# Two fused attention blocks on one core: layer norms, context loads and row tests moved between engines

## The chip, the cores and the metric

The kernel runs on one core of a Trainium2 chip. The core has a matrix engine (TensorE, PE in the profile; its weight loads are shown as PEld), a vector engine (VectorE, DVE), an activation engine (ScalarE, ACT), a general engine (GpSimd, POOL) and a sync engine (SyncE, SP), from whose queue nearly all DMAs of this kernel are issued. [...] Every engine works through its own queue in order, and engines wait for each other through semaphores. The metric is the device time of one execution in microseconds; a time is given as the median of several runs.

## What is computed

Sixteen sequences of 256 rows and 512 columns go through two transformer blocks. All arithmetic is in float32.

```python
# block 0
q = layer_norm(x) @ q_w ; k, v = split(layer_norm(ctx) @ kv_w)      # 16 heads of 32
x = x + softmax(q k^T * scale, masked) v @ proj_w + proj_b
x = x + gelu(layer_norm(x) @ fc1_w + fc1_b) @ fc2_w + fc2_b         # 512 -> 2048 -> 512
# block 1
mask0 = 1 - all(x == 0, axis=2)
x1 = layer_norm(x + mha(x, x, mask0, causal)) * g1 + b1
mask1 = 1 - all(x1 == 0, axis=2)
x2 = layer_norm(x1 + mha(x1, ctx, mask1)) * g2 + b2
z = (relu(x2 @ f1^T + b) * mask0 @ f2^T + b') * mask0
out = layer_norm(x2 + z) * g3 + b3
```

Two details matter below. `mask0` and `mask1` ask of every row whether it has a nonzero element. In the cross attention the context rows are multiplied with `mask1` before keys and values are made of them.

## The kernel before

**Tiling.** The sixteen sequences are worked on as eight groups (`NG`), each of two sequences, that is 512 rows, or four tiles (`G`) of 128 rows by 512 columns. A float32 product is made of three matmuls over a high and a low part (`mm3`); hence each operand is first "split": one engine copies it to the rounded high part and DVE or POOL subtracts to get the low part (`split`, L127 to L133; `split_lazy`, L139 to L142).

**Stages in order of time.** First comes block 0's attention (up to about 690 us). Then comes the first MLP (`Mlp0`): its first half "up" (512 to 2048, to about 1082 us) and its second half "down" (2048 to 512, to about 1458 us), both with a Strassen scheme of seven products, where sums of quarter matrices replace the eighth product. Block 1 follows: eight self attention jobs (job 0 to 7, about 66 us each), eight cross attention jobs (job 8 to 15, about 76 us each) and the second MLP from about 2600 us.

**The order of work.** PE's order is written out by hand (`tc.manual_schedule(engines={PE})`). On the other engines' queues and on SP the framework places the instructions when the kernel is built, by a simulated time line and by the program's order. In attention, `weave` interleaves two streams on PE: the attention of one job (scores, transposes of the exponentials, weighted sums) and the `feed` of the next job (its projections, transposes of its input rows, and the loads of weights). So `feed(8)`, which prepares the first cross job, runs beside the attention of job 7.

**Norms in block 1.** When half a job (one sequence) is done, two calls of `norm` are put in a list, and one of them is emitted per head. `norm` calls `layer_norm(..., True)`: the statistics on DVE (L238 to L241), the power -0.5 on POOL (L242), then the normalizing in one DVE pass (L252) and gain and offset in two POOL passes (L253, L254). For a self job DVE then tests the row for nonzero elements (`nonzero`, L1225, with an output tile `junk` that nobody reads), which gives `m1`. Then the rows are stored to DRAM (L1298). The third norm, in the second MLP, uses the two fused DVE passes L256 and L257 instead.

**Context rows.** `context(n, t)` loads tile t of the context (L1408), multiplies it by `m1` on POOL (L1409) and has PE transpose it (L282). It is called in the feed of a cross job: tiles 0 and 1 after the first of four projections, tile 2 after the second and tile 3 after the third (`FRONTS`). The row tiles `cx` share the three buffers of the tag `t512` with `junk` and, in the second MLP, with `relu` and `y`.

**The first MLP, down.** It runs over 32 steps: four per group of rows (q = 0 to 3), each with seven products of twelve matmuls. In each step `sums_down` makes four sums for the next step: `differences` puts s1 and s3 on POOL (L796, L798) and s2 and s4 on DVE (L797, L799). After each product its operand slot is rewritten for the next step (`write`: a copy on ACT, L141, and a subtraction on DVE, L142). The residual rows `x` are loaded at q = 1 (q = 2 in the first group), and the second bias is added to them on POOL (`offset`, L1042) at q = 2 (q = 3 in the first group). In a group's last step `end` adds the products into these rows on DVE and POOL; it then stores them and tests each of the four row tiles for nonzero elements with `nonzero` on DVE, into `m0`.

**The first MLP, up.** Its four sums per group go through the same `differences`. At its start (`begin`) all four sums and the seven low parts are made on POOL, and the high parts by DVE copies (L860).

## Time and profile before

| What | us |
|---|---|
| median of three runs (2823.62 to 2831.68) | 2824.41 |
| the profiled execution | 2834.77 |
| its span, first to last instruction | 2832.9 |
| PE idle between matmuls, down (1082 to 1458) | 34.1 |
| the same, cross attention (1970 to 2600) | 42.2 |
| the same, up (690 to 1082) | 24.0 |
| the same, self attention (1482 to 1970) | 4.4 |

The idle times are sums of PE's gaps above 0.15 us in the trace. The mean granted clock of PE is 0.981 of full speed. In the profile an engine's line reads: line of the code, engine, operation, output<-inputs, shapes and count; in a list of waits it reads "who waited <- for whom: us in total, times, longest". In a timeline the first two columns are the start in us and the length, and brackets at the end give the idle time of the engine just before, with what ended it. `SPq` marks the issue of a DMA, not its transfer. An idle engine costs nothing unless it makes the end later.

### The profile page before, as it was taken

What the parts mean: (1) busy time and instruction counts of PE and PEld (TensorE: products, weight loads), DVE (VectorE), ACT (ScalarE), POOL (GpSimd) and SP (SyncE); (2) the same over time, 40 slices, a digit from 0 to 9 for tenths busy, and PEclk for the clock granted to TensorE, in tenths of its full rate; (3) what the DMA queues carried; (4) which work ended last, traced back from release to release, by engine and by line L of the source; (5) the groups of instructions that cost most, each with busy time, mean ns of one, the idle gap of its engine ahead of it and who ended that gap; (6) DMA issues with size and microseconds to landing.
All of it is one profiled execution on the core that took longest, in us unless ns stands there. A gap on an engine that the chain in (4) does not pass through costs nothing.

```text
span 2832.9 us, 56614 instructions
## 1 busy us (share of the span) xinstructions
PE 2683.6 (95%) x18970; PEld 2261.0 (80%) x18970; DVE 2047.1 (72%) x5801; ACT 1794.4 (63%) x5221; POOL 942.1 (33%) x963
## 2 busy tenths in 40 slices
PE   7999999998899999899989999999889999999998
PEld 5777777776799999899977888887767777777787
DVE  7666666757746568888876777777667777777887
ACT  4877777778455555333337878787667777777532
POOL 6122211204501125545551222335233323324533
PEclk9999999999999999999999999999999999999999
DMA  7565555654323344434366565667556555556321
GB/s 229 168 192 177 174 176 168 193 157 139 128 110 132 120 149 164 149 120 150 132 230 189 180 190 182 191 197 238 160 187 193 174 182 185 176 161 181 99 93 60
DMA packets 287809, 465.41 MB, mean 164 GB/s; under 512 B 36256, under 2 KB 188320, under 8 KB 279328
## 3 DMA queue, kind: packets, MB, share of 16 engines
q1 hardware_dynamic: 287520, 461.78, 51.3%
q8 instruction: 153, 2.51, 0.4%
q14 instruction: 136, 1.11, 0.1%
HBM read 284.97 MB, written 176.69 MB: 163 GB/s over the span
## 4 chain that ended last, share of the span: by engine, by line
PE 70%; DVE 13%; DMA 6%; issue 4%; ACT 3%; POOL 3%; SPq 0%; POOLq 0%; DVEq 0%; ACTq 0%
PE ps_p L263 18%; PE ps_v L263 15%; PE ps_pt L454 9%; PE ps_z L473 6%; PE ps_s L413 5%; PE down L1025 5%; PE up_sc L912 4%; DVE c_t L142 3%; PE up_pt L912 2%; PE up_mm L912 2%; PE ps_t L282 2%; ACT e L438 1%; DMA d<-qk 1%; DVE st L238 1%; PE ps_e L1253 1%
## 5 line engine op out<-in xcount | busy, mean ns | idle before, releaser
L438 ACT ACTIVATE e<-e,mn 128x256 f32<-128x256 f32 (+1 forms) x1024 | 487.7, 480 | 69.3 <-DVE mn L428 67.7
L460 ACT COPY pt<-ps_pt 128x512 f32<-128x512 f32 (+1 forms) x696 | 378.0, 546 | 161.8 <-PE ps_pt L454 150.7
L454 PE MATMUL ps_pt<-ident,e 128*128 128x128 f32 x2816 | 437.4, 274 | 11.7 <-ACT pt L460 6.0
L454 PEld LDWEIGHTS ps_pt<-ident,e 128*128 128x128 f32 x2816 | 336.7, 141 | 52.3 <-ACT pt L460 12.4
L413 PE MATMUL ps_s<-stack 97*128 97x256 f32 (+1 forms) x1536 | 331.7, 297 | 16.8 <-ACT e L438 13.3
L413 PEld LDWEIGHTS ps_s<-stack 97*128 97x128 f32 (+1 forms) x1536 | 269.0, 190 | 72.6 <-ACT e L438 18.3
L1329 POOL TENSOR_TENSOR x<-x,zz 128x256 f32<-128x256 f32 x128 | 95.5, 746 | 592.5 <-DVE zz L1322 577.5
L438 ACT ACTIVATE e<-ps_s,mn 128x256 f32<-128x256 f32 x512 | 241.0, 483 | 79.1 <-DVE mn L424 50.2
L1025 PE MATMUL down<-w_h,c_t 128*128 128x256 f32 x900 | 261.8, 292 | 24.0 <-DVE c_t L142 24.0
L1025 PE MATMUL down<-w_h,x_t 128*128 128x256 f32 x868 | 252.5, 291 | 9.4 <-ACT x_t L141 7.8
L1025 PE MATMUL down<-w_l,x_t 128*128 128x256 f32 x868 | 251.3, 289 | 0.0
L428 DVE CUSTOM_DVE_ANT_0 e<-mb,ps_s 128x256 f32<-128x256 bf16 x512 | 192.7, 415 | 77.8 <-PE ps_s L413 75.7
L242 POOL TENSOR_TENSOR rstd<-rstd,nhalf 128x1 f32<-128x1 f32 x192 | 123.3, 649 | 332.9 <-DVE rstd L241 286.4
L473 PE MATMUL ps_z<-pt,v 128*32 128x256 f32 (+1 forms) x3072 | 212.3, 376 | 10.1 <-DVE zs L651 3.6
L263 PE MATMUL ps_p<-x_t,q_h 128*128 128x512 f32 x640 | 217.0, 420 | 3.6 <-DVE x_t L133 1.7
L424 DVE TENSOR_REDUCE mn<-ps_s 128x2 f32<-128x512 f32 x256 | 174.9, 683 | 51.4 <-PE ps_s L413 48.3
L428 DVE CUSTOM_DVE_ANT_0 e<-tri,ps_s 128x128 f32<-128x128 f32 (+1 forms) x512 | 158.6, 345 | 61.2 <-PE ps_s L413 58.9
L1025 PEld LDWEIGHTS down<-w_h,c_t 128*128 128x128 f32 x900 | 178.3, 198 | 27.6 <-DVE c_t L142 27.6
L438 ACT ACTIVATION_READ_ACCUMULATOR e<-e,mn 128x1 f32 x1024 | 197.8, 193 | 0.0
L141 ACT CAST x_t<-sums 128x512 fp32r<-128x512 f32 x152 | 90.4, 618 | 154.4 <-DVE sums L797 84.6
L1025 PEld LDWEIGHTS down<-w_h,x_t 128*128 128x128 f32 x868 | 172.6, 199 | 11.6 <-ACT x_t L141 9.8
L473 PEld LDWEIGHTS ps_z<-pt,v 128*32 128x32 f32 x3072 | 86.0, 111 | 115.0 <-issue 29.4
(248 smaller groups left out, 7632.0 us busy)
## 6 DMA issues: line engine op xcount, KB each, us to landing
stack<-d SPq DMA_DIRECT2D x1152, 128.0 KB
d<-qk SPq DMA_DIRECT2D x192, 512.0 KB
hid<-ho SPq DMA_DIRECT2D x32, 1024.0 KB
raw<-hid SPq DMA_DIRECT2D x32, 1024.0 KB
x<-xd SPq DMA_DIRECT2D x128, 256.0 KB
xd<-x SPq DMA_DIRECT2D x96, 256.0 KB
xin<-in_x_dram SPq DMA_DIRECT2D x32, 256.0 KB
xin<-in_ctx_dram SPq DMA_DIRECT2D x32, 256.0 KB
```

What stands on the lines that cost most here:

```text
L242: nc.gpsimd.tensor_tensor(out=rstd[:, 1:2], in0=rstd[:, 0:1], in1=nhalf, op=ALU.pow)
L263: nc.tensor.matmul(ps, w[p], x[q], start=(k == 0 and i == 0), stop=(k == kc - 1 and i == 2))
L413: nc.tensor.matmul(ps[:, t, :], u.st[: self.rows, 0, j, ts(t, P)], u.st[: self.rows, 1, j, :], start=True, stop=True,)
L424: nc.vector.tensor_reduce(mn, ps, AX.X, ALU.min)
L428: nc.vector.tensor_tensor_reduce(out=e[:, at], in0=bias[t], in1=ps[:, t, : job.width[t]], scale=-SC, scalar=BIG, op0=ALU.add, op1=ALU.min, ...
L438: nc.scalar.activation(e[:, at], ps[:, t, :] if bias is None else e[:, at], AF.Exp, bias=mn[:, t : t + 1], scale=-1.0, accum_out=u.rs[:, t ...
L454: nc.tensor.transpose(pp[:, ts(x, P)], e[:, at : at + P], ident)
L460: nc.scalar.copy(pt[:, :n], pp[:, :n])
L473: nc.tensor.matmul(z[ts(j, D), w[0] * P :], job.v[u.i * NT + mc][:, u.c * P + j * D : u.c * P + (j + 1) * D], u.pt[j][:, x0 * P : (x0 + le ...
L912: nc.tensor.matmul(ps[:, mm, :], w[p][:, k, :], x[q][:, k, :], start=(first and mm == k == j == 0), stop=(k == 1 and j == 2), skip_group_c ...
L1025: nc.tensor.matmul(ps[:, t, :], x[p][:, mm, ts(t, P)], w[r][:, bo, :], start=(q == mm == t == j == 0), stop=(q == self.NS - 1 and mm == 1 ...
L1329: nc.gpsimd.tensor_tensor(out=xv, in0=xv, in1=zz, op=ALU.add)
```

## The change

It has several parts, in all of which the results stay the same up to rounding:

- `layer_norm` loses its pooled form. The norms of block 1 take two fused passes on DVE: (x - mean) * gain, then x * rstd + offset.
- Context rows are loaded by a new function `context_rows`, apart from `context`. After the keys of a job's feed, tiles 0 to 2 of the next job are loaded if that is a cross job, or tiles 0 and 1 if it is the first cross job. Inside `context(n, t)`, once tile t is transposed, tile t + 3 is loaded. A tile not yet loaded is loaded just before its use.
- `Mlp0.end` no longer calls `nonzero`. ACT takes the absolute values of a row tile and accumulates their sum into `m0`; one DVE operation on four columns then turns the sums into 0 or 1.
- In `differences` s4 goes to POOL in every case.
- `offset` is called at q = 3 for all groups.
- `write` in `begin` copies the high part on ACT instead of DVE, and subtracts on POOL as before.

```diff
-    def layer_norm(pool, x, gain, offset, pooled=False):
+    def layer_norm(pool, x, gain, offset):
         mean, rstd = ln_stats(pool, x)
-        if pooled:
-            nc.vector.tensor_scalar(x, x, mean, rstd, ALU.subtract, ALU.mult)
-            nc.gpsimd.tensor_tensor(out=x, in0=x, in1=gain, op=ALU.mult)
-            nc.gpsimd.tensor_tensor(out=x, in0=x, in1=offset, op=ALU.add)
-        else:
-            nc.vector.scalar_tensor_tensor(x, x, mean, gain, ALU.subtract, ALU.mult)
-            nc.vector.scalar_tensor_tensor(x, x, rstd, offset, ALU.mult, ALU.add)
+        nc.vector.scalar_tensor_tensor(x, x, mean, gain, ALU.subtract, ALU.mult)
+        nc.vector.scalar_tensor_tensor(x, x, rstd, offset, ALU.mult, ALU.add)
...
             own.tensor_tensor(out=s2, in0=s1, in1=a11, op=ALU.subtract)
             pool.tensor_tensor(out=s3, in0=a11, in1=a21, op=ALU.subtract)
-            own.tensor_tensor(out=s4, in0=a12, in1=s2, op=ALU.subtract)
+            pool.tensor_tensor(out=s4, in0=a12, in1=s2, op=ALU.subtract)
...
-            if own is None:
-                split_lazy(self.a[i], h, l, nc.vector)
-            else:
-                nc.vector.tensor_copy(h, self.a[i])
-                own.tensor_tensor(out=l, in0=self.a[i], in1=h.bitcast(F32), op=ALU.subtract)
+            split_lazy(self.a[i], h, l, own or nc.vector)
...
                 for t in range(G):
                     junk = self.flat("junk").rearrange("p m n -> p (m n)")
-                    nonzero(junk, x[:, t, :], m0[:, g, t : t + 1])
+                    nc.scalar.activation(
+                        junk, x[:, t, :], AF.Abs, accum_out=m0[:, g, t : t + 1]
+                    )
+                nc.vector.tensor_scalar(m0[:, g, :], m0[:, g, :], 0.0, None, ALU.not_equal)
...
-                elif q == (2 if g else 3):
+                elif q == 3:
                     self.offset(xs[g])
...
-                layer_norm(pool, x, table[:, 0, :], table[:, 1, :], True)
+                layer_norm(pool, x, table[:, 0, :], table[:, 1, :])
...
+        cxs = {}
+
+        def context_rows(n, t):
+            if n < len(jobs) and jobs[n].cross and (n, t) not in cxs and t < G:
+                cx = cxs[n, t] = pool.tile([P, C], F32, tag="t512", name="cx", bufs=3)
+                nc.sync.dma_start(out=cx, in_=of("ctx", jobs[n].g)[:, t, :])
+
         def context(n, t):
...
-            cx = pool.tile([P, C], F32, tag="t512", name="cx", bufs=3)
-            nc.sync.dma_start(out=cx, in_=of("ctx", job.g)[:, t, :])
+            cx = cxs[n, t]
             nc.gpsimd.tensor_scalar(cx, cx, job.m[:, t : t + 1], None, ALU.mult)
-            return transposed(job.c_t, cx, t)
+            cost = transposed(job.c_t, cx, t)
+            context_rows(n, t + 3)
+            return cost
...
                     for t in FRONTS[c]:
+                        context_rows(n, t)
                         yield context(n, t)
...
             weight(n + 1, "k")
+            for t in range(3 if n + 1 > NG else 2):
+                context_rows(n + 1, t)
```

## The prediction

> **What bounds the kernel now.** I read the page's busy shares first, then the waits of TensorE, then busy time and granted clock by stage, and then the timeline at the longest waits. PE is busy for 2683.6 of 2832.9 us, so only a shorter PE idle time, or a higher granted clock, can shorten the run.

> ```profile
> PE 2683.6 (95%) x18970; PEld 2261.0 (80%) x18970; DVE 2047.1 (72%) x5801; ACT 1794.4 (63%) x5221; POOL 942.1 (33%) x963
> ...
> PE ps_t L282 <- POOL cx L1409: 24.6, 2, 12.9
> PE down L1025 <- DVE c_t L142: 24.0, 16, 3.5
> PE ps_s L413 <- ACT e L438: 13.3, 7, 2.7
> ...
> 1082.00:1458.00 376.00, 342.46 (x2697) 336.48 (x2696) 321.95 (x406) 140.00 (x244) 203.07 (x144) 0.96 0.41 141
> 1482.00:1970.00 488.00, 483.17 (x3493) 390.91 (x3492) 359.72 (x1677) 381.67 (x1331) 143.57 (x155) 1.00 0.64 196
> 1970.00:2090.00 120.00, 95.37 (x674) 75.58 (x673) 74.29 (x271) 72.99 (x242) 45.77 (x43) 0.89 0.58 184
> 2090.00:2600.00 510.00, 491.88 (x3505) 387.56 (x3505) 381.56 (x925) 368.49 (x1197) 166.21 (x168) 0.99 0.59 178
> ```

> The stage rows give length, busy PE, PEld, DVE, ACT and POOL, the granted clock, DMA. They are the first MLP's second half ("down"), the self attention jobs, the change from self to cross attention, and the cross jobs. Self attention is full: 483 of 488 us. PE's three longest waits lie in the other three stages, all of which the change touches.

> At the change of stages PE stands still twice, for 11.75 us (at 1978) and 12.88 us (at 2052). The first in detail:

> ```profile
> 1976.01 2.71 POOL L253 TENSOR_TENSOR x<-x,ln 128x512 f32<-128x512 f32 x2
> ...
> 1981.14 2.48 POOL L254 TENSOR_TENSOR x<-x,ln 128x512 f32<-128x512 f32 x2
> ...
> 1982.72 1.26 SPq L1298 DMA_DIRECT2D xd<-x  x2
> 1984.04 0.90 SPq L1408 DMA_DIRECT2D cx<-in_ctx_dram  x2
> ...
> 1988.15 3.11 POOL L1409 TENSOR_SCALAR cx<-cx,m 128x512 f32<-128x512 f32 x2 [3.31 <-DMA cx<-in_ctx_dram]
> ...
> 1989.77 1.12 PE L282 MATMUL ps_t<-ident,cx 128*128 128x128 f32 x4 [11.75 <-POOL cx L1409]
> ```

> POOL finishes a norm's gain and offset (L253, L254); SP can then issue the norm's store; only behind it in SP's queue comes the load of the context rows; 4.1 us later POOL masks them, and PE transposes them. In cross jobs a small version occurs once a job:

> ```profile
> 2297.20 1.57 POOL L1409 TENSOR_SCALAR cx<-cx,m 128x512 f32<-128x512 f32 x1 [6.12 <-PE ps_pt L454]
> 2298.74 1.18 POOL L242 TENSOR_TENSOR rstd<-rstd,nhalf 128x1 f32<-128x1 f32 x2
> ...
> 2299.33 2.19 DVE L252 TENSOR_SCALAR x<-x,mv,rstd 128x512 f32<-128x512 f32 x2 [2.00 <-POOL rstd L242]
> ...
> 2303.29 0.50 PE L413 MATMUL ps_s<-stack 97*128 97x256 f32 x2 [2.15 <-ACT e L438]
> ...
> 2306.00:2308.00 2.00, 2.00 (x15) 0.88 (x8) 1.22 (x3) 1.02 (x4) 2.00 (x3) 0.50 0.91 344
> ```

> The context load was issued at 2292.94, POOL's queue waits for it, the norm's rstd waits behind it, DVE's normalizing stands in front of the next scores' minimum, and PE starves. The last row shows the price added: the clock is 0.50 after the stall, from about 2304.7 to 2308.1, so 3.4 us at half speed lose another 1.7 us.

> [...] the split's subtraction (L142) takes 0.68 us alone and about 1.75 us beside POOL's additions. [...]

> **The change part by part.**

> *Norms of block 1 (64).* Per norm it removes a DVE tensor_scalar (L252, mean 0.875 us) and two POOL operations (1.31 and 1.32), and adds two DVE fused passes. The third norm uses the same passes: L256 and L257 have medians of 0.742 and 0.750, 1.49 together (means 0.986 and 0.799, next to POOL). So DVE +0.6 us, POOL -2.6 us each; 64 norms give DVE +40, POOL -168 us. The first pass doesn't need rstd, so DVE no longer waits for POOL before it. The store leaves earlier: by the two POOL operations of two norms, 5.2 us, plus a wait of 2.0 us behind a weight cast. What pays is the score work behind DVE in 16 pairs of self norms, where PE has no slack (gaps of 0.24 us a job now) and 16 pairs of cross norms. From below: nothing, since the passes mix with the score work. From above: 2 us idle plus clock. I take 0.2 us a pair: +6.

> *Context rows.* For jobs 9 to 15 three row tiles are loaded before the previous job's values, half a job ahead; for job 8 two are, the third is still issued where it was, behind the norm's stores, and the fourth after the first transposes. The second long stall goes: 12.88 and 2.2 for the clock (half speed until about 2069), 15. Of the first, the norm's earlier store is what helps: the load at about 1977 instead of 1984, so 7 of 11.75 go (bounds 3 and 14). Once-a-job stalls: 1.45, 2.08, 2.15, 2.68, 2.08, 2.48 = 12.9, plus 1.7 for the clock on five = 8.5, sum 21; other work may be late next, I take 16 (bounds 5 and 21). The tiles share three buffers (t512) with the self norms' zero test. The last two self norms find them held until job 9's first transposes; their test is then late on DVE, and it is needed only by job 15. SP's issue of a fourth tile waits for transposes, with the stores of q and the stack loads behind it; these come later in PE's order too, so I cost it nothing.

> *First MLP, down.* PE idles 34.1 us here and its clock is 0.96, so 8% of 376 us at half speed, up to 15 more. A group (g) takes 44.7 us, from stall to stall; 84 products of 0.123 us by four steps make 41.4. Two stalls repeat:

> ```profile
> 1233.31 0.67 DVE L1225 TENSOR_SCALAR_CACHE_REDUCE junk<-x 128x512 f32<-128x512 f32 x1
> ...
> 1233.91 0.68 DVE L797 TENSOR_TENSOR sums<-sums,raw 128x512 f32<-128x512 f32 x1
> ...
> 1237.06 0.39 PE L1025 MATMUL down<-w_h,c_t 128*128 128x256 f32 x1 [1.25 <-DVE c_t L142]
> ...
> 1240.98 2.54 POOL L1042 TENSOR_TENSOR x<-x,b_fc 128x512 f32<-128x512 f32 x2 [8.75 <-DMA x<-xd]
> 1243.48 1.29 POOL L796 TENSOR_TENSOR sums<-raw 128x512 f32<-128x512 f32 x1
> ```

> Four zero tests (0.60 us each, start to start) stand before the sum that DVE owes; two bias additions stand before POOL's first sum, and 2.76 us of idle PE follow at 1250.59. The tests go to ACT: 32 at 0.62 (as its 128x512 copies) and 0.2 for the accumulator (as L438's) = 0.8; ACT is busy 140 of 376 us, and its queue holds casts that may come 1 us later. s4 goes from DVE (L799, mean 1.21) to POOL (about 1.3): DVE -39, POOL +42 us for 32. The bias additions move one step later in seven groups, into the step that also has POOL's four output additions. [...] So of 4.0 idle and 1.3 clock a group, at most 2.5 can go; I take 1.75, times eight: -14 (bounds +10 and -25).

> *The rest.* The up half moves seven s4 likewise[...]: 0 (-4 to +4). Seven early casts go from DVE to an ACT idle for 7.67 us; DVE L860 stood before L651, for which PE waited 3.25 us: -2 (0 to -4). Eight `not_equal` on four columns: nothing beside 0.14 us operations; DVE has idle time there.

> Sum: -7 -15 -16 -14 -2 +6 = -48. The profiled execution took 2834.8 us (span 2832.9), 10.4 over the median 2824.4, and the differences apply to both: 2786.8 profiled, 2776.4 as median.

> **The rivals.**
> (a) The loads stay late, since other queue entries precede them, and only quicker norms help: first stall -3, second -5, job stalls 0, down -14, rest as above: -18, 2806. For: the order on SP and DVE is made anew at build. Against: the loads are put half a job earlier in program order, and trace order stays near it.
> (b) Down gains nothing[...]: -34 + 0, or +10 there: about 2795. [...] Against: the stalls follow particular queued operations, which leave.
> (c) Slower: the fused passes hold up the scores at 32 norm pairs. Each idles PE by 1 us and then costs a part of the clock, 1 us: 64 us against 54 gained, 2834. It decides from 1.7 us a pair. For: PE is 99% busy in self jobs, DVE 74%. Against: the score buffers now ride out a pair's 1.75 us of L252 with 0.24 us idle, and this grows only to 3.0.
> (d) Gains and new stalls cancel: 2824.

> **How the numbers follow.** Forecast 0.52, (a) 0.13, (b) 0.17, (c) 0.11, (d) 0.07. Faster 0.82; within 0.3% (8.5 us, about what a measurement can tell from no change) 0.07; slower 0.11. With the favourable bounds (first stall -14, job stalls -21, down -25, the rest -4, passes 0) the sum is -79, 2745; I end the range at 2752, and above at 2820, which takes in (a) and (b).

> **What would show it.** Right: no wait of PE for cx over 6 us; cross jobs of about 73 us instead of 76 to 78; the clock in 1970:2090 above 0.95; POOL 110 to 130 us less busy; groups of down at about 43 us. Wrong: new PE waits for mn or e (L413) at norm pairs; ACT's Abs in front of a cast that PE waits for; down at 45 us or more.

## The result, and the profile after

| | us |
|---|---|
| before, median of 6 runs on the same chip (2823.62 to 2833.0) | 2825.69 |
| after, median of 6 runs (2810.48 to 2816.37) | 2814.32 |
| ratio, 95% interval | 0.9953 [0.9938, 0.9968] |
| profiled execution, before and after | 2834.77 and 2812.60 |

The change saves 11.4 us. The forecast was 2776.4, a saving of 48: the direction held and the range (2752 to 2820) holds the time, but the saving is a quarter of what was forecast. The profiled pair shows 22 us, because the profiled execution of before lies 9 us above its median and that of after 2 us below.

The busy line of the page of after comes first.

```profile
PE 2676.1 (95%) x18970; PEld 2259.4 (80%) x18970; DVE 2045.4 (73%) x5763; ACT 1823.0 (65%) x5292; POOL 862.1 (31%) x874
```

POOL is 80 us less busy (862 against 942), and PE is busy for 2676 us instead of 2684, in a span that is 22 us shorter. So two thirds of the difference between the two profiled executions are PE's idle time. These are some of PE's waits in after, whole run:

```profile
PE down L1015 <- DVE c_t L142: 21.5, 16, 2.3
...
PE ps_pt L449 <- DVE lbias L1255: 10.0, 9, 3.9
PE down L1015 <- ACT x_t L141: 8.8, 6, 2.0
PE ps_s L408 <- ACT e L433: 7.1, 15, 1.2
```

Of the three waits that led the list before, the one for `cx` (24.6 us) has shrunk to 2.5. The waits of the down products are as large as before: 21.5 and 8.8 against 24.0 and 7.8. A new wait of 10.0 us for `lbias` has come. It is the bias tile that `lengths` makes from a count of nonzero columns, and it stood nowhere in the forecast. By stage, in the same windows and columns as before:

```profile
1082.00:1458.00 376.00, 340.22 (x2641) 334.66 (x2639) 314.22 (x317) 151.88 (x291) 254.89 (x171) 0.94 0.40 139
1482.00:1970.00 488.00, 474.16 (x3415) 382.54 (x3413) 359.43 (x1670) 379.53 (x1306) 83.08 (x100) 1.00 0.63 194
1970.00:2090.00 120.00, 113.47 (x810) 90.22 (x809) 88.49 (x315) 87.65 (x296) 34.98 (x35) 0.99 0.69 210
2090.00:2600.00 510.00, 496.85 (x3583) 394.29 (x3581) 395.32 (x972) 378.49 (x1223) 113.10 (x121) 1.00 0.58 181
```

Down (first row) has a lower clock than before, 0.94 against 0.96, with 52 us more of POOL. Self attention (second row) has 9 us less of busy PE, with 78 instructions fewer in the window. The change of stages (third row) is the clear gain: PE 113 of 120 us instead of 95, at a clock of 0.99 instead of 0.89.

Windows fixed in time shift against the work. PE's order is the same in all kernels here, so the time between the starts of the same two of its 18,970 instructions measures a stage exactly, for the one execution that was profiled. "MLP kernels" are those below with the attention left as it was (seven profiles), "norm kernels" those with the fused norms (nine, after among them).

| stretch (PE instructions) | before | after | other profiles |
|---|---|---|---|
| up (4444 to 7268) | 373.6 | 369.7 | 373.0 to 376.1 where up is unchanged, 369.4 to 371.7 where it is changed |
| down (7480 to 10120) | 375.3 | 378.8 | 370.6 to 383.7 where down is unchanged |
| start of block 1 (10120 to 10470) | 53.6 | 55.9 | 53.3 to 53.6 with the tests on DVE, 54.7 to 58.1 on ACT |
| self jobs (10470 to 13350) | 397.8 | 402.2 | MLP kernels 396.7 to 400.6, norm kernels 399.3 to 402.2 |
| around the first long stall (13350 to 14000) | 102.0 | 100.5 | see below |
| around the second (14000 to 14450) | 78.6 | 67.8 | 65.9 to 68.2 in all kernels with the new row loads |
| cross jobs (14450 to 18000) | 516.7 | 503.0 | MLP kernels 507.9 to 509.7, norm kernels 502.7 to 506.8 |

The last row has a surprise: the cross jobs of before, unchanged, took 7 to 9 us less in every one of seven other profiles. Some 4 to 5 us of this are longer stalls in the one trace of before. PE also stood at half clock there for 10.2 us, against 0 to 3.4 in the seven; the last section shows what went before it.

### The profile page after: what moved, and what is told of

Read it like the earlier page. It is cut to its first block, busy times and chain, and to the rows that moved or that the text cites. A ratio compares the mean times of both kernels' runs of the same rounds, so it can differ in the third digit from the quotient of the medians.

```text
span 2810.9 us, 56659 instructions
## 1 busy us (share of the span) xinstructions
PE 2676.1 (95%) x18970; PEld 2259.4 (80%) x18970; DVE 2045.4 (73%) x5763; ACT 1823.0 (65%) x5292; POOL 862.1 (31%) x874
## 4 chain that ended last, share of the span: by engine, by line
PE 67%; DVE 15%; DMA 7%; issue 4%; ACT 3%; POOL 3%; SPq 1%; POOLq 0%; DVEq 0%; ACTq 0%
PE ps_p L258 17%; PE ps_v L258 14%; PE ps_pt L449 8%; PE down L1015 5%; PE ps_s L408 5%; PE ps_z L468 5%; PE up_sc L902 3%; DVE c_t L142 3%; PE up_pt L902 2%; PE up_mm L902 2%; PE ps_t L277 2%; DVE st L238 1%; DMA xd<-x 1%; ACT e L433 1%; DVE e L423 1%
## 5 line engine op out<-in xcount | busy, mean ns | idle before, releaser
L1015 PE MATMUL down<-w_h,c_t 128*128 128x256 f32 x900 | 264.5, 295 | 21.5 <-DVE c_t L142 21.5
L242 POOL TENSOR_TENSOR rstd<-rstd,nhalf 128x1 f32<-128x1 f32 x192 | 140.6, 738 | 316.6 <-DVE rstd L241 314.4
L468 PE MATMUL ps_z<-pt,v 128*32 128x256 f32 (+1 forms) x3072 | 200.1, 369 | 4.3 <-ACT pt L455 2.1
L1015 PEld LDWEIGHTS down<-w_l,x_t 128*128 128x128 f32 x868 | 175.0, 202 | 0.0
```

The source lines that it names most:

```text
L242: nc.gpsimd.tensor_tensor(out=rstd[:, 1:2], in0=rstd[:, 0:1], in1=nhalf, op=ALU.pow)
L468: nc.tensor.matmul(z[ts(j, D), w[0] * P :], job.v[u.i * NT + mc][:, u.c * P + j * D : u.c * P + (j + 1) * D], u.pt[j][:, x0 * P : (x0 + le ...
L1015: nc.tensor.matmul(ps[:, t, :], x[p][:, mm, ts(t, P)], w[r][:, bo, :], start=(q == mm == t == j == 0), stop=(q == self.NS - 1 and mm == 1 ...
```

## The experiments

All ratios are to the kernel before, run in turn on the same chip (medians of before: 2824.6, 2825.3, 2826.8 and 2826.4 in the four sets), with 95% intervals.

### The parts: which half pays

The attention half (fused norms and row loads), the MLP half (Abs tests, s4 on POOL, `offset`, early casts), and the two parts of the attention half alone. Each edit is the part of the diff above that bears its name.

> Only the two parts in block 1 (fused norms, context rows), the first MLP as before. Theory 1, from the aligned traces: block 1 gives about 25 us and the first MLP gives 6 back, so this kernel is about 18 us faster than before (ratio 0.9935) and some 6 us faster than the whole change. Rival: the first MLP gives nothing back and the 8 us lost in down are a matter of one execution; then this kernel equals the whole change (ratio 0.9953).

> Only the parts in the first MLP (abs on ACT, s4 on POOL, offset at q = 3, early copies on ACT). Theory 1: about 6 us slower than before (ratio 1.002), PE idle in 1082 to 1458 at 36 us or more, and the clock there at 0.94. Rival: same as before within 2 us. The forecast had it 16 us faster (0.9943).

> Only the fused norms on DVE. Theory 1: they shorten the first long wait for cx (11.75 us) to about 5 us, since the store in front of the context load leaves earlier, and the six waits of 2 us in cross jobs by half; they cost about 5 us in the self jobs: 5 to 12 us faster (ratio 0.9965). Rival: most of the gain in block 1 comes from them, not from the loads: 15 us or more.

> Only the context rows loaded ahead, norms as before. Theory 1: the second long wait for cx (12.88 us and 2 us of clock) goes, the six in cross jobs go, the first stays at about 10 us: 18 us faster (ratio 0.9935), no cost in the self jobs before 1900 us. Rival: the norm's two POOL passes still stand before the masking on POOL, so the waits stay at half: 8 us or less.

| kernel | median us | ratio | saved |
|---|---|---|---|
| attention half | 2812.33 | 0.9959 [0.9946, 0.9971] | 11.6 |
| norms alone | 2819.78 | 0.9987 [0.9979, 0.9995] | 3.7 |
| rows alone | 2815.10 | 0.9966 [0.9957, 0.9976] | 9.6 |
| MLP half | 2824.65 | 0.9996 [0.9985, 1.0007] | 1.1, not told from nothing |

("Saved" is one less the ratio, times 2825.) The theories for these four were read from one pair of profiles, and were off every time: 18, 5 to 12 and 18 us for the three parts in block 1, a loss of 6 for the MLP half. The net gain is the attention half's. Its parts add up within the intervals: 3.7 and 9.6 against 11.6. PE's waits for `cx` show what each part does to the two long stalls, which were 11.75 and 12.88 us. First the waits of the kernel with rows alone, then of that with norms alone:

```profile
PE ps_t L282 <- POOL cx L1415: 13.4, 2, 11.9
```

```profile
PE ps_t L282 <- POOL cx L1409: 15.1, 2, 10.9
...
PE ps_pt L454 <- DVE lbias L1262: 9.3, 10, 3.3
```

With the rows alone one stall of 11.9 us is left: the first. The second has gone, and the stretch around it is 65.9 us instead of 78.6; the stretch around the first is 105.2, 3 us longer than before. With the norms alone the first has shrunk to 4.1 us, yet its stretch is as long as before: 102.0 us. In its place PE waits 3.3 us for `lbias`, 2.1 us for `qk` and 0.8 us for a smaller tile, so that PE's waits in this stretch have fallen only from 13.0 to 10.8 us. So the norms' gain lies elsewhere, in the cross jobs: PE's wait for `e` there, from 2095 to 2600 us, in a kernel with unchanged attention (f2_up, below) and with norms alone:

```profile
PE ps_s L413 <- ACT e L438: 8.1, 6, 1.5
```

```profile
PE ps_s L413 <- ACT e L438: 3.6, 9, 0.8
```

Six stalls of up to 1.5 us, once a job, have become nine short ones. With rows alone all of them stay, and the cross jobs took 514.2 us in that profile. So it is the norms that remove them. This fits the chain that the prediction read: from 1482 to 2600 us DVE's norms wait 12.2 us for `rstd` in before and 3.7 us in after, since the first fused pass doesn't need it.

### The MLP half: a gain in up, a loss in down

> Only the up half's parts of the MLP edit: s4 on POOL in up's differences (down's stay on DVE), and the early casts of write on ACT. Theory: up is 4 to 6 us shorter in all profiles that have this, stalls 1.50 to 0.97 us in each of seven groups, and it stays so when nothing else is changed: 2819 to 2821, ratio 0.998. Rival: what up gains, down gives back since its first groups wait for something else: 2824, ratio 1.000.

> Only down's s4 on POOL instead of DVE (32 of them). Theory: s4 stands on POOL behind two bias additions of 128x512[...], so the wait of PE for the split after it grows by about 2 us in each of seven groups and crosses into half clock: 5 to 12 us slower, ratio 1.002 to 1.004. Rival (the prediction's own step): DVE relieved by 1.2 us a step, down shorter by some 3 to 6 us: ratio 0.998 to 0.999.

> Only the row tests of the first MLP: sums of absolute values on ScalarE and one comparison a group, instead of 32 VectorE reductions. Theory: the stall of 1.25 us for the split behind the four tests goes in each group, with a part of the half clock after it, 8 x 1 us, and 2 to 4 us are lost at the start of block 1, where the last group's tests stand on ACT before the first casts: 2818 to 2822, ratio 0.998 to 0.999. Rival: PE then waits for the other input of the same step, POOL's sums, and nothing is gained in down, the loss at block 1's start stays: 2826 to 2828, ratio 1.001.

The first has the early casts of the diff above as well, the third its lines with Abs and `not_equal`. In the first two `differences` takes the engine of s4 as an argument, GpSimd for one half of the MLP and VectorE for the other:

```diff
-            own.tensor_tensor(out=s4, in0=a12, in1=s2, op=ALU.subtract)
+            last.tensor_tensor(out=s4, in0=a12, in1=s2, op=ALU.subtract)
```

| kernel | median us | ratio |
|---|---|---|
| up: s4 on POOL, early casts on ACT | 2818.18 | 0.9980 [0.9973, 0.9988] |
| down: s4 on POOL | 2833.87 | 1.0038 [1.0025, 1.0051] |
| down: tests as Abs on ACT | 2832.44 | 1.0026 [1.0015, 1.0038] |

Up gains 5.7 us, as expected, and each of down's two moves costs 7 to 11. The Abs kernel was expected to gain; the s4 kernel came out in its expected range, but for another reason. (`offset` called at q = 3 has no part in this: the program that it gives has the same instructions in the same order on every engine, and POOL's order in down is the same in the trace of the MLP half, which has it, and in that of the kernel with Abs and s4 alone, which hasn't.) The timeline of the Abs kernel at one group's change shows why Abs loses:

```profile
1241.96 2.54 POOL L1042 TENSOR_TENSOR x<-x,b_fc 128x512 f32<-128x512 f32 x2 [8.22 <-DMA x<-xd]
1244.46 1.29 POOL L796 TENSOR_TENSOR sums<-raw 128x512 f32<-128x512 f32 x1
1245.71 1.27 POOL L798 TENSOR_TENSOR sums<-raw 128x512 f32<-128x512 f32 x1
1245.79 1.75 DVE L797 TENSOR_TENSOR sums<-sums,raw 128x512 f32<-128x512 f32 x1 [6.55 <-POOL sums L796]
1246.94 3.39 POOL L1042 TENSOR_TENSOR x<-x,b_fc 128x512 f32<-128x512 f32 x2
...
1248.29 0.39 PE L1025 MATMUL down<-w_h,x_t 128*128 128x256 f32 x1 [1.92 <-ACT x_t L141]
1249.14 1.75 DVE L799 TENSOR_TENSOR sums<-raw,sums 128x512 f32<-128x512 f32 x1
...
1251.54 0.58 PE L1025 MATMUL down<-w_h,c_t 128*128 128x256 f32 x1 [2.74 <-DVE c_t L142]
```

The stalls behind the four tests (0.78 and 1.25 us in most groups) are gone, as forecast. But POOL stands for 8.22 us in front of two bias additions whose rows haven't landed, with s1 queued behind them, and DVE stands for 6.55 us waiting for s1. As PE comes to this place sooner while the rows come when they did, PE now waits 1.92 and 2.74 us, and its clock is half afterwards. That the rows set the time shows group by group: from the start of a group's first addition to PE's first matmul behind the second stall it takes 9.61 to 9.72 us in the second to seventh group of before and 9.57 to 9.66 in the Abs kernel, whatever PE did until then. So the end of the second stall follows the rows, and time that PE saves ahead of it can't be kept. In the row of this kernel for the next 4 us the clock is the third number from the end:

```profile
1252.00:1256.00 4.00, 4.00 (x21) 4.00 (x21) 2.83 (x6) 0.13 (x1) 1.98 (x2) 0.50 0.35 121
```

PE stood at half clock for 47.8 us of down in this kernel, against 27.3 in before. The start of block 1, behind the last group's tests, is 1.1 us longer as well (54.7 against 53.6).

The s4 kernel loses at another place, at the end of a group:

```profile
1263.79 1.74 POOL L799 TENSOR_TENSOR sums<-raw,sums 128x512 f32<-128x512 f32 x1
...
1268.52 1.78 DVE L142 TENSOR_TENSOR c_t<-raw,x_t 128x512 fp32r<-128x512 f32 x1
1270.22 0.68 DVE L1069 TENSOR_TENSOR x<-x,down 128x512 f32<-128x512 f32 x1
1271.05 0.36 PE L1025 MATMUL down<-w_h,x_t 128*128 128x256 f32 x1 [1.07 <-DVE x L1069]
1271.52 2.26 SPq L1075 DMA_DIRECT2D xd<-x  x4
...
1279.32 1.74 SPq L1037 DMA_DIRECT2D x<-xd  x4
1280.04 0.39 PE L1025 MATMUL down<-w_h,c_t 128*128 128x256 f32 x1 [1.73 <-DVE c_t L142]
```

s4 (L799) and, behind it, the output additions keep POOL busy beside DVE's splits, which take up to 1.78 us there (0.68 us in median over down in before); so DVE's addition of a product (L1069), for which PE waits 1.07 us, comes late (before has this wait in the first group alone). PE's wait behind the tests has grown from 1.25 to 1.73 us. In this kernel the second stall is in most groups under 1 us; the expectation had the loss there. The two SP lines show why the rows come late: a group's rows go into the same single buffer (tag `x1`) as those of the group before, and their load (L1037) is issued only when the stores of those (L1075) are done. From 1130 to 1440 us of before SP waits 40.0 us for these stores, in 14 waits.

The whole change shows the place of the second stall with s4 on POOL as well (its timeline):

```profile
1236.56 2.55 POOL L1032 TENSOR_TENSOR x<-x,b_fc 128x512 f32<-128x512 f32 x2 [5.86 <-DMA x<-xd]
1239.07 1.28 POOL L790 TENSOR_TENSOR sums<-raw 128x512 f32<-128x512 f32 x1
1240.39 1.76 DVE L791 TENSOR_TENSOR sums<-sums,raw 128x512 f32<-128x512 f32 x1 [6.13 <-POOL sums L790]
1241.56 3.39 POOL L1032 TENSOR_TENSOR x<-x,b_fc 128x512 f32<-128x512 f32 x2
1242.07 1.76 DVE L142 TENSOR_TENSOR c_t<-raw,x_t 128x512 fp32r<-128x512 f32 x1
1243.75 4.04 DVE L142 TENSOR_TENSOR c_t<-sums,x_t 128x512 fp32r<-128x512 f32 x3
1244.92 1.72 POOL L793 TENSOR_TENSOR sums<-raw,sums 128x512 f32<-128x512 f32 x1
1245.56 0.58 PE L1015 MATMUL down<-w_h,c_t 128*128 128x256 f32 x1 [2.15 <-DVE c_t L142]
```

DVE waits 6.13 us for s1. The second pair of additions takes 3.39 us beside DVE's operations, where the first took 2.55 us, and PE waits 2.15 us for the second split. That subtraction takes 1.76 us here, beside POOL's additions; the same takes 0.68 us at 1247.71, where POOL stands idle. s4 (L793) now runs behind the additions and no longer stands in front of that split; the Abs kernel's wait, with s4 there, was 2.74 us.

Do the two losses add up, and what does down cost within the whole?

> Down's two moves together, row tests on ScalarE and s4 on GpSimd, without up's part (e2_mlp less f2_up). Alone they gave 1.0026 and 1.0038. Theory: both hit the same place, the sums behind the two bias additions on GpSimd, and what counts there is the later of the two waits, so the losses don't add: e2_mlp (0.9996) over f2_up (0.998) leaves 1.0016, 2826 to 2832. Rival: the losses add, 1.0064, 2841 to 2846, and up's part must then gain far more in e2_mlp than alone.

> The change without its down part: norms, context rows, up's s4 and early casts; down's row tests and s4 stay on VectorE, the bias additions on GpSimd as before. Theory: the prediction's step for down failed in sign, down's part costs about 4 us net, and up's part gains 7: 2803 to 2808, ratio 0.993 to 0.9945, against 0.9953 of the whole change. Rival: the stages influence each other and the whole change loses nothing by down: 2812 to 2816, ratio 0.995 to 0.9965.

Abs and s4 together in down: 2830.68 us, 1.0017 [1.0010, 1.0023]. The losses don't add. With the tests off DVE the s4 kernel's waits at the end of a group are gone or at most 0.9 us in all groups but the first, and with s4 off DVE the Abs kernel's stall of 2.74 us is one of 2.15. The change without its down part: 2807.47 us, 0.9936 [0.9922, 0.9951], shorter than the whole change with its 0.9953. Both times came out as the theory said. The two intervals of 0.9936 and 0.9953 overlap, so the cost of down's part is shown by the direct comparison, 1.0017, and not by this one.

### Is it the bias additions in front of the sums?

> Row tests of the first MLP on ScalarE as in e5_abs (2832.4 us, ratio 1.0026), and the bias additions of offset (4 of 128x512 a group) on VectorE instead of GpSimd; nothing else. Theory: what e5_abs lost is the order on GpSimd: two bias additions, which wait for the residual's transfer, stand in front of the sums that PE needs next; DVE stands idle for 6.55 us at that place, waiting for these sums, and has room for four additions of 0.6 us. PE's two waits there (1.92 and 2.74 us) and the half clock after them go, seven times, some 4 to 6 us each: 2790 to 2804, ratio 0.988 to 0.993. Rival: VectorE now waits for the same transfer with its splits behind it, and PE waits for them in the same place: 2825 to 2833, ratio 1.000 to 1.003.

> Only the bias additions of offset on VectorE instead of GpSimd, the row tests as before on VectorE. Theory: the second stall of a group (1.3 to 2.8 us in the kernel before) goes with a part of the half clock, the first (0.78 and 1.25 us, behind the tests) stays: 2808 to 2816, ratio 0.994 to 0.997. Rival: with tests and additions VectorE is the bound and nothing is gained: 2825 to 2830, ratio 1.000 to 1.002.

```diff
-                nc.gpsimd.tensor_tensor(
+                nc.vector.tensor_tensor(
                     out=x[:, t, :], in0=x[:, t, :], in1=self.b_fc2, op=ALU.add
                 )
```

With this and Abs: 2814.09 us, 0.9960 [0.9946, 0.9975]. With this alone: 2815.91 us, 0.9957 [0.9942, 0.9971]. So moving four additions a group away from POOL turns the Abs kernel's loss of 7 us into a gain of 11 us. If the two moves simply added, they would give 0.9983 (1.0026 and 0.9957); the measured 0.9960 is less, and beside additions on DVE the tests' move costs nothing (0.9960 against 0.9957). That the additions' place was the cause of the loss follows from this only just outside the noise, and the traces show the way. The size was overrated, however (0.988 to 0.993 was expected), and the tests' move to ACT gains nothing even now. The timeline of the kernel with both has the reason:

```profile
1284.32 0.69 DVE L1042 TENSOR_TENSOR x<-x,b_fc 128x512 f32<-128x512 f32 x1 [3.71 <-DMA x<-xd]
...
1286.39 1.51 DVE L1042 TENSOR_TENSOR x<-x,b_fc 128x512 f32<-128x512 f32 x1 [0.18 <-DMA x<-xd]
1287.83 1.75 DVE L142 TENSOR_TENSOR c_t<-raw,x_t 128x512 fp32r<-128x512 f32 x1
1289.64 0.39 PE L1025 MATMUL down<-w_h,c_t 128*128 128x256 f32 x1 [1.88 <-DVE c_t L142]
```

Here DVE waits 3.71 us for the same transfer of the residual rows, with the splits that PE needs behind the additions. Part of the rival was right: the wait has moved with the additions. PE comes behind the stall 8.4 to 8.8 us after the first addition now, instead of 9.6. A load of these rows some microseconds earlier would be the next thing to try. It wasn't tried; it needs a second buffer for the rows, since the one that they have is held until the stores of the group before are done.

### What took the place of the first long stall

> Norms and context rows as in e1_attention (ratio to the kernel before 0.9959, 2812.3 us), and one more buffer for the length bias tile lbias (three instead of two). Theory: the fused norms delay the length chain on DVE, so that its copy waits for the small transfer of the tile two lengths back, and PE then waits for lbias (8.1 us of PE's waits from the self jobs' start to the end of the cross jobs in e1_attention, 3.9 of it at the change of stages; the kernel before has none). With the third buffer these waits go and 6 to 9 us with them: 2803 to 2807, ratio 0.993 to 0.994. Rival: the chain is late because DVE is full, and another operation of the same chain (qk, the scores' minimum) is what PE waits for next: within 2 us of 2812, ratio 0.995 to 0.997.

> As f1_lbias (2810.4 us, 0.9949), with the four maskings of the first cross job's context rows on VectorE instead of GpSimd. Theory: the first long stall was replaced by a wait for GpSimd: three maskings of 1.57 us, now early, stand in front of the key weights' casts and subtractions there, and a copy of the turned weights (pt) needs the staging buffer that these free (4.23 us of PE's wait), and a masking itself is late for 2.3 us. On VectorE they free GpSimd, and 4 to 8 us go at the change of stages: 2803 to 2807, ratio 0.992 to 0.9935. Rival: the weights' transfers are late, not the casts, and the wait stays: 2809 to 2812, ratio 0.994 to 0.9955.

```diff
-        bias = pool.tile([NB * HPC, S], F32, tag="lbias", name="lbias")
+        bias = pool.tile([NB * HPC, S], F32, tag="lbias", name="lbias", bufs=3)
```

```diff
-            nc.gpsimd.tensor_scalar(cx, cx, job.m[:, t : t + 1], None, ALU.mult)
+            own = nc.vector if n == NG else nc.gpsimd
+            own.tensor_scalar(cx, cx, job.m[:, t : t + 1], None, ALU.mult)
```

A third buffer for `lbias` gives 2810.43 us, 0.9949 [0.9937, 0.9961]. That is 2 to 3 us from the attention half's 0.9959, less than the two intervals tell apart, and short of the 6 to 9 expected. The waits at the change of stages (1930 to 2060 us) in this kernel say why:

```profile
PE ps_z L473 <- ACT pt L460: 4.2, 1, 4.2
PE ps_t L282 <- POOL cx L1415: 2.3, 1, 2.3
PE ps_p L263 <- DVE qk L128: 2.1, 1, 2.1
```

The wait of 3.9 us for `lbias` has gone, and one of 4.2 us for `pt` stands in its place. Its timeline:

```profile
1951.98 1.57 POOL L1415 TENSOR_SCALAR cx<-cx,m 128x512 f32<-128x512 f32 x1 [6.99 <-DMA cx<-in_ctx_dram]
1953.51 0.61 POOL L187 CAST k_h<-wst 128x512 fp32r<-128x512 f32 x1
1954.15 1.56 POOL L1415 TENSOR_SCALAR cx<-cx,m 128x512 f32<-128x512 f32 x1
...
1956.91 1.26 POOL L190 TENSOR_TENSOR k_l<-wst,k_h 128x512 fp32r<-128x512 f32 x1
1958.21 0.48 ACT L460 COPY pt<-ps_pt 128x384 f32<-128x384 f32 x1 [3.98 <-POOL k_l L190]
```

`pt` and the staged weights `wst` share six buffers (tag `pts`). The copy waits until POOL has made the low part of a weight, and in front of that, on POOL, stand maskings of context rows, which now come early, and a weight's cast waits behind them. With the masking of the first cross job on DVE the time is 2805.17 us, 0.9929 [0.9912, 0.9946], and the stretch around the first long stall is 96.0 us instead of 101.2: a gain of 5 us, as expected. (The two ratios, from different sets, overlap. The stretch is the better witness: in the three profiles with the third buffer and all masking on POOL it is 99.5 to 101.2 us, in the two with the first cross job's masking on DVE 96.0 and 97.5.) In that kernel the wait for `pt` is gone, `cx` costs 0.9 and 0.6 us, and a wait for `lbias` of 2.4 us is back:

```profile
PE ps_pt L454 <- DVE lbias L1262: 2.4, 1, 2.4
PE ps_p L263 <- DVE qk L128: 2.1, 1, 2.1
```

### What gains, together

> All that has gained alone: norms, context rows, the third buffer of lbias (together f1_lbias, 2810.4 us), up's s4 and early casts (f2_up, 7 us less), and row tests on ScalarE with the bias additions on VectorE (g1_abs_off). Theory: the gains lie in different stages and add up: 2810.4 - 7 - (25 to 30) = 2773 to 2780 if g1_abs_off gives what its theory says, ratio 0.982 to 0.985. Rival: down gains nothing, and only the other parts add: 2803, ratio 0.992.

> As g3_best but with the row tests left on VectorE as before. Theory: the tests' move pays only once the bias additions are out of the way, then by 5 to 12 us: this one takes 2782 to 2792, ratio 0.985 to 0.989, longer than g3_best. Rival: the move of the tests is worth nothing or costs, in down or at the start of block 1: this one is as short as g3_best or shorter.

> As g4_noabs (2797.6 us, 0.9892), with the same maskings on VectorE. Theory: the gain of h3_mask adds: 2791 to 2795, ratio 0.987 to 0.9885. Rival: no gain, 2796 to 2800, ratio 0.989 to 0.9905.

| kernel | median us | ratio |
|---|---|---|
| norms, rows, third `lbias`, up's part, Abs, additions on DVE | 2799.94 | 0.9905 [0.9889, 0.9921] |
| the same without Abs | 2797.64 | 0.9892 [0.9875, 0.9909] |
| and the first cross job's masking on DVE | 2791.53 | 0.9881 [0.9864, 0.9897] |

The gains of different stages add up: what the third `lbias` kernel, up's part and Abs with the additions gave alone makes 0.9889 for the first row, and without Abs 0.9886 for the second. The 2773 to 2780 us expected for the first had counted 25 to 30 us for down. Abs is worth nothing here either: the rival was right in g4_noabs. The start of block 1, behind the last group's tests, is 53.3 us without Abs and 58.1 with it. The time of the last kernel is as expected, but its ratio and that of the row above overlap, and in the two profiles the stretch of the masking is only 2 us shorter; down, which is the same in both, is 5 us shorter. The last kernel beats before by 34.9 us, and the change by about 20 (0.9881 against 0.9953). Its stages, down and the change of stages:

```profile
1082.00:1458.00 376.00, 349.66 (x2713) 339.64 (x2712) 337.04 (x464) 141.52 (x249) 166.09 (x121) 0.97 0.45 156
...
1970.00:2090.00 120.00, 115.27 (x838) 91.40 (x837) 92.32 (x296) 89.49 (x296) 26.41 (x26) 1.00 0.65 196
```

## Why the prediction was right in direction and wrong in size

| step | forecast | what the runs show |
|---|---|---|
| second long stall | -15 | -9.6 timed (rows alone); its stretch -10.8 |
| first long stall | -7 | none: its stretch 102.0, with the norms 102.0, with the rows 105.2, with norms and rows 101.4 (100.5 in after) |
| once-a-job stalls | -16 | about -4 (cross jobs 508.7 on average in the MLP kernels, 504.3 in the norm kernels) |
| down | -14 | +4.8 (1.0017, with the start of block 1) |
| early casts and up | -2 | -5.7 (0.9980) |
| the fused passes' cost | +6 | about +2.4 (self jobs 398.2 and 400.6 on average in the same two sets) |

The right-hand column adds up to about -12, against the measured -11.4. Several of its terms come from stretches of single executions, so some of this agreement may be chance.

**Down failed in sign, and it is the step that failed most.** The prediction put "of 4.0 idle and 1.3 clock a group, at most 2.5 can go; I take 1.75, times eight". The 2.5 was the author's estimate, from a sum of POOL's and DVE's work in a group as if the two never overlapped. The step took the two stalls of a group as separate, each owed to the operations queued in front of it. The first did go with the tests. But the second is set by a time that doesn't move: when the residual's rows land (PE comes behind it 9.6 us after the first addition, with and without Abs). What PE saved ahead of it was waited for there, at the price of half the clock (47.8 us of down in the Abs kernel, against 27.3 in before). The step also counted on `offset` moving, which it doesn't; it took s4 on POOL for a relief, where DVE's splits beside it take up to 1.78 us at the end of a group; and it left out the start of block 1, 1 to 5 us longer behind tests on ACT. The groups of after take 45.7 to 47.5 us, where the prediction hoped for 43; in before they take 44.6 to 47.1, and it had taken one of the shortest, 44.7, for all. For down, rival (b), "down gains nothing", was nearest, but its reason was that same estimated sum, which wasn't shown to be the limit: the order and the wait for the rows were. Its bound of +10 holds the +4.8. That rival (a) lies nearest in the total, 2806 against 2814, is luck, as its reason fell.

**The first long stall** shrank as the prediction said, from 11.75 to about 2 us. The step failed where it took the stall's shrinking for time. The waits for `lbias`, `qk` and, behind `lbias`, for a weight's buffer were next, 9 to 11 us of waits in all where there had been 13, and the prediction named none of them: it put what stands next in the other queues at nothing.

**The once-a-job stalls** were taken from one execution: 2.08 to 2.68 us in five jobs, plus clock. The clock was misread: "1.7 for the clock on five" makes 8.5, but the trace of before has half clock behind three of the five (2304.6, 2458.2 and 2536.7 us, 3.4 us each), which makes 5.1. Six other profiles of the same cross jobs have 7.6 to 8.5 us of stalls in all, against 12.9, and at most one step of half clock. What could be had was half of what was counted, and "the differences apply to both" (the profiled execution and the median) was wrong by just this. It was the norms that removed them, not the rows' loads.

**Rightly read:** the second long stall, its cause and its cure, with 10 us instead of 15; the fused passes at 0.740 and 0.736 us in median (0.742 and 0.750 were taken); the clock of the change of stages, 0.99, with 0.95 named as the mark; that Abs takes 0.617 us and its accumulator 0.187, against 0.8 together (with it the trace has three table loads, as before). Rival (a), "the loads stay late", fell, and so did (c): in after no wait of 1 us for a score's minimum (`mn`) has come at the norm pairs; those that came are of 0.3 to 0.5 us. POOL was to fall by 110 to 130 us and fell by 80, since the s4 that it got in down take 1.73 us in median instead of 1.3, and its other operations there stretch too (3.39 us for a pair of bias additions, against 2.55).

## What to carry to other kernels

A stall goes for good only if nothing is late just behind it: before its length is booked as gain, look for the next thing whose time is fixed by a transfer, and ask what stands behind it in its engine's queue. An operation that waits for a DMA, placed in front of work that others need, costs its wait and not its length (POOL stood for 8.22 us in front of two additions of 1.27 us each); here four additions of 0.7 us a group, moved to another engine, were worth 12 us of the run. And measure a stall in more than one execution before you count it: a stall repeated once a job had 12.9 us in one profile and about 8 in six others.

## What was not expected of the hardware

The length of a stall doesn't alone decide on the clock. Of two stalls of 2.08 us in the cross jobs of before, at 2227.0 and 2457.5 us, the first left the clock at full speed and the second halved it; one of 2.68 us, at 2381.3, left it full as well. The stretches behind the two:

```profile
2227.00:2229.00 2.00, 1.97 (x15) 1.37 (x15) 2.00 (x4) 1.37 (x4) 2.00 (x2) 1.00 0.13 40
...
2459.00:2461.00 2.00, 2.00 (x17) 1.12 (x19) 2.00 (x5) 1.49 (x5) 2.00 (x3) 0.50 0.77 244
```

| stall ends at | its length | PE idle in the grid steps that it touches | clock then |
|---|---|---|---|
| 2227.0 | 2.08 | 1.14 and 0.94 | full |
| 2303.3 | 2.15 | 2.11 | half |
| 2381.3 | 2.68 | 1.06 and 1.62 | full |
| 2457.5 | 2.08 | 2.08 | half |
| 2535.1 | 2.48 | 0.67 and 1.81 | half |

So half clock followed here when enough of a stall fell into one step. Over the two traces, without the first 100 and the last 20 us, there are 1,535 steps at full clock, and 30 of them were followed by half clock. Every one in which PE idled for 1.79 us or more was, and none with less than 1.62 us; between the two figures both occur (1.62 us was followed by half clock in before, 1.69 us by full clock in after). That is about half a step. Short stalls in one step count together: two of 0.82 and 1.26 us behind the tests of before fell into one step, 2.07 us in all, and the clock was half from 1147.5 us on for 3.4 us. So of two stalls of 2.08 us in one execution, one cost 1.7 us more (3.4 us at half speed) and the other nothing more.

Unchanged code also varied between executions: down, not touched, took between 370.6 and 383.7 us in different profiles, with a group's second stall at 1.5 to 2.0 us in most groups of one (the third `lbias` kernel) and at 2.75 us in most groups of another (the attention half).
